# A conditional transformer block on one core: the last ssm residual gets second-level leaves, sums of the last ff residuals move ahead, the last stores are cut by column halves

## The chip, the cores and the metric

The kernel runs on one core of a Trainium2 chip. The core has a matrix engine (PE, which also loads its weights, PEld), a vector engine (DVE), a scalar engine (ACT), GpSimd (POOL) and a sync engine (SP). Each runs its own queue in program order; semaphores order them against each other. In this kernel PE writes to eight PSUM tiles ("banks") of up to 128 x 512 floats, DVE and ACT read them, and POOL works on SBUF alone. Transfers are issued from SP and ACT. The metric is device microseconds per execution, as the median of several runs.

## The reference

The input is x, 2 sequences of 2048 tokens with 512 features, and one condition vector per sequence. All is in float32:

```
emb = silu(t) @ ada_w + ada_b            # six vectors of 512 per sequence
shift_msa, scale_msa, gate_msa, shift_mlp, scale_mlp, gate_mlp = split(emb, 6)
norm = ln(x) * (1 + scale_msa) + shift_msa
h = gelu(norm @ ssm_w1 + ssm_b1)         # 512 -> 512, exact gelu
x = x + gate_msa * (h @ ssm_w2 + ssm_b2) # the "ssm residual"
norm2 = ln(x) * (1 + scale_mlp) + shift_mlp
hf = gelu_tanh(norm2 @ ff_w1 + ff_b1)    # 512 -> 1024
x = x + gate_mlp * (hf @ ff_w2 + ff_b2)  # 1024 -> 512, the "ff residual"
```

## The kernel before

**Tiling.** The 4096 tokens are cut into 8 blocks of 512 (`i` = 0 to 7). A block's x is one tile of 128 partitions x 4 token rows x 512 features. For each block there are four matmul stages, named after the tiles they write: hA (first ssm layer), oA (ssm residual), hC (first ff layer) and oC (ff residual). Names like `px_hC` or `pl_oC_P_y` are PSUM tiles of such a stage. The loop over `i` does hC_i, oA_(i+1), oC_i, hA_(i+2); block 5 ("ahead", `i + 3 == NBLK`) has the order hC_5, oA_6, hA_7, oC_5, oA_7. Blocks 6 and 7 ("alone") have hC and oC only. PE goes through all stages in one row; all other work is hooked into these stages: `hook(hooks, places, ops)` puts an operation behind a named place of a stage, and it lands in its own engine's queue in that order. The order is written out by hand (`tc.manual_schedule()`).

**Seven products instead of eight.** A matrix product cut into 2 x 2 quarters is done with seven quarter products P1 to P7, whose operands are sums and differences of quarters (`sums_of_first` for activations, `sums_of_second` for weights, four additions each; the third works in place). The results are added up in PSUM: `BANK` says which bank (y, x or v) a product goes to. After a product is complete, DVE adds the bank into the quarters of x that need it; a later product accumulates onto the same bank, and so waits until that read is done. After P1, ACT copies bank y to bank x in the `CARRIED` order. hC uses a program of 26 products (`HK_P`), whose moving operands ("registers", `forms`) are made by the 20 operations of `HK_B`, most on POOL, six of them on DVE from copies in PSUM.

**Leaves.** A product can be cut again in the same way: seven leaf products with 128-wide operands instead of four matmuls with 256-wide ones. `residual_with_leaves` (from L912) does so for oA of blocks 3 to 6: P1, P5, P6, P7 plain, and P2, P3, P4 in seven leaf rounds R0 to R6 (products in the order of `LEAVES`); a round does the same leaf of all three. Their activation operands are made by `First.leaf_sums`, eight sums, their weight operands by `leaves_of_w2`, which changes w2 in place. `plain_w2` changes it back for oA_7, which is done by `residual` (L876) with seven plain products, 28 matmuls of 128 x 256.

`residual_in_leaves` (from L977) does oC of blocks 1, 4, 6 and 7: P1 and P6 plain, P2, P3, P5, P4, P7 as leaves, each of two matmuls. Its order is P1 and its read (L1005), round R0, plain P6, rounds R1 to R6. After round 1 DVE reads P6 for the upper half of x (L1005), after round 2 for the lower half (L1092). Each round's results are added at L1056. In round 6 of the last block the order is P4, P7, P2, P3, P5. oC of blocks 2, 3 and 5 is `residual_in_all_leaves`; its adds are at L1150.

**Operands of the ff residual.** `Second.summed(1, ...)` makes the four hC sums of the second half of the ff activations (`hC_sums`), `Second.leaf_sums` the leaf operands: `sums24` (for P2, P4), `sums35` (P3, P5) and `sums7` (P7), four each. For blocks 6 and 7 `hC_sums` and `sums24` are on DVE, the others on POOL. All these additions are at L386.

**Statistics.** The normalisation of a block's x starts with `stats` (four pairs at L608 and L609), then `root` (L661 on DVE, L662 on POOL), then `steps`. Those of the last block stand partly in oA_7 and partly between the products of hC_6.

**Stores.** In the last block's oC two token rows are stored after each of the last three rounds, one from SP, one from ACT (L1103, L1106): after rounds 4 and 6 half of their columns, after round 5 whole rows.

Of the kernel before, what the change touches and what calls it, by code (L numbers as in the profile page):

```python
# [140 lines left out]
def kernel(  # L141
# [371 lines left out]
    def plain_w2(w_sb, s, eng):  # L513

        for w in (w_sb[:, KD // 2 :, :], s[:, 2]):
            v = w.rearrange("p h (q e d) -> p h q e d", e=2, d=P)
            eng.tensor_tensor(v[:, 0, :, 1], v[:, 1, :, 1], v[:, 0, :, 1], ALU.subtract)

# [393 lines left out]
    def residual_with_leaves(name, i, hops, wops, leaf_wops, hooks):  # L912
# [7 lines left out]
        rooms = {  # L920
            b: (ps_t if tag == "t" else ps_g).tile([P, 4, P], F32, tag=tag, name=f"pl_{name}_{b}")
            for b, tag in (("y", "t"), ("x", "x"), ("v", "t"))
        }
        started = set()
# [15 lines left out]
        def leaf_round(r):  # L940
            f = LEAVES[r]
            b = LEAF_BANK[f]
            for n, p in enumerate(("P2", "P3", "P4")):
                nc.tensor.matmul(
                    rooms[b][:, n, :],
                    hops.leaves[p][f],
                    leaf_wops[p][f],
                    start=b not in started,
                    stop=(f in ("P2", "P3", "P4")),
                    skip_group_check=True,  # L950
                )
                started.add(b)
            if r == 0:
                nc.scalar.copy(rooms["x"][:, :3], rooms["y"][:, :3])
                started.add("x")
                return
            t, e = LEAF_AT[f]
            for d, n in ((X[:, 0, t, :, e, :], slice(0, 2)), (X[:, 1, t, :1, e, :], slice(2, 3))):
                nc.vector.tensor_tensor(d, rooms[b][:, n], d, ALU.add)
# [17 lines left out]
    def residual_in_leaves(name, i, hops, wops, leaf_wops, kdim, hooks, last, five, carried):  # L977
# [84 lines left out]
        for r, f in enumerate(LEAVES):  # L1062
# [11 lines left out]
            if r == 0 and carried:  # L1074
                x23, x4 = rooms["P23", "x"], rooms["P4", "x"]
                nc.scalar.copy(x23[:, :2], rooms["P23", "y"][:, :2])
                nc.scalar.copy(x4[:, : 1 + five], rooms["P4", "y"][:, : 1 + five])
                if five:
                    nc.scalar.copy(x4[:, 2], seeded[:, 0])
                started |= {("P23", "x"), ("P4", "x")}  # L1080
                dests = {}
            for p in ("P5", "P4", "P7", "P3") if i + 2 == NBLK and r == 5 else on:
                if p in dests:
                    add(*dests[p])
            if five and r == 0:
                hooked("R0")
                run(plain("P6"))
                hooked("P2")
            if five and r == 1:
                read("P6", "12")  # L1090
            if five and r == 2:
                nc.vector.tensor_tensor(  # L1092
                    xt[:, 2:4, :].rearrange("p t (q d) -> p t q d", q=2),
                    ps["y"].unsqueeze(2).to_broadcast([P, 2, 2, F]),
                    xt[:, 2:4, :].rearrange("p t (q d) -> p t q d", q=2),
                    ALU.add,
                )
            if not five and r == 4:
                read("P7", "22", "21")
            if last and r >= 4:  # L1100
                for eng, row in ((nc.sync, t), (nc.scalar, 2 + t)):
                    if f == "P3":
                        eng.dma_start(out=out_blk[i][:, row, :], in_=xt[:, row, :])  # L1103
                    else:
                        cols = slice(e * P, (e + 1) * P)
                        eng.dma_start(  # L1106
                            out=out_blk[i][:, row].rearrange("p (q d) -> p q d", q=2)[:, :, cols],
                            in_=xt[:, row].rearrange("p (q d) -> p q d", q=2)[:, :, cols],
                        )
# [99 lines left out]
    class First:  # L1209
# [14 lines left out]
        def leaf_sums(self, eng):  # L1224

            flat = forms.rearrange("p n a r -> p (n a r)")[:, 18 * P : 27 * P]
            s24 = thirds(flat[:, : 6 * P].rearrange("p (s q t) -> p s q t", s=3, q=2))
            s3 = thirds(flat[:, 6 * P :].rearrange("p (s t) -> p s t", s=3))
# [387 lines left out]
    for i in range(1, NBLK):  # L1616
# [31 lines left out]
        elif nxt:  # L1648
            hook(hooks, (1, 3), last_stats[2:])
            hook(hooks, (3,), [n2[i + 1].root])  # L1650
# [37 lines left out]
        hook(hooks, EARLY, hC_sums[: 2 if alone else 4])  # L1688
# [63 lines left out]
        if alone:  # L1752
            hook(hooks, ("P1",), hC_sums[2:] + sums7[:2] + sums35[:2] + sums24[:2] + sums7[2:] + sums35[2:])
            hook(hooks, ("R0", "P6"), sums24[2:])
        if seven and nx2:
            n1_sums = hA[i + 2].summed(nc.gpsimd) if ahead else n1[i + 2].summed(nc.gpsimd)
            hook(hooks, ("0a",), [lambda: n2[i + 1].root()] + sums17[:1] + (leaf_fold or [])[:-2])
# [11 lines left out]
        elif nx2:  # L1769

            hook(hooks, ("P1",), [lambda: n2[i + 1].root()])
            hook(hooks, ("P1",), (leaf_fold or [])[:-2] + [lambda: n2[i + 1].rest(found["room"])])
# [3 lines left out]
            if leaf_fold:  # L1776
                hook(hooks, ("P5", "P7"), leaf_fold[-2:])
# [97 lines left out]
        if ahead:  # L1875
# [3 lines left out]
            plain_w2(w2_sb, w2_s, nc.vector)  # L1879
            residual(f"oA_{i + 2}", i + 2, hA[i + 2], w2_ops, KD // 2, hooks, order=CARRIED)  # L1880
# [47 lines left out]
```

## Time and profile before

| what | us |
|---|---|
| median of 3 runs (lowest, highest) | 580.98 (580.52, 581.02) |
| the profiled execution | 580.38 |
| its span, first to last instruction | 578.6 |
| PE busy in the span | 572.1 |
| DVE, POOL, ACT busy | 453.8, 432.2, 292.8 |
| oA_7 on PE | 471.5 to 483.6 |
| hC_6 and oC_6 on PE | 483.6 to 528.7 |
| hC_7 and oC_7 on PE | 528.7 to 574.5 |

The granted PE clock is full in every slice of the page. A row of the time order gives the start (us from the start of the span), the length, the engine, the line, the operation, the tiles written and read, the shape and the count; a length for several instructions runs from the first one's start to the last one's end. A bracket at the end of a row gives the idle time of the engine before it and who ended it. PE's ends are modelled and overlap the next start, so distances on PE are taken from start to start. One matmul in float32 counts as two instructions. A windows row gives, behind the window, its length, the busy time of PE, PEld, DVE, ACT and POOL with the count of instructions, the PE clock, the busy share of the DMA engines and GB/s.

### The profile page before, as it was taken

Reading aid. Unit: us, or ns where it says so; the run is one execution under the profiler, and the core shown is the slowest. Engines: PE = TensorE matmul, PEld = TensorE weight load, DVE = VectorE, ACT = ScalarE, POOL = GpSimd, SP = SyncE. Lnnn points to the kernel's source line nnn. Section 1 sums busy time; section 2 is a strip of 40 time slices with the busy share of each in tenths; the row PEclk is TensorE's granted clock in tenths of the full one; section 3 lists DMA queues with packets and bytes.
Section 4 is the critical chain, followed back from the end, with each engine's and each line's share of the span. In section 5 each row is a group of like instructions: output and inputs, shape, how many; then the busy total and the mean of one; then the engine's idle time right before and its main releaser. Section 6 shows DMA issues by size and latency. Waiting matters only on the chain.

```text
span 578.6 us, 10061 instructions
## 1 busy us (share of the span) xinstructions
PE 572.1 (99%) x3425; PEld 514.2 (89%) x3425; DVE 453.8 (78%) x955; ACT 292.8 (51%) x574; POOL 432.2 (75%) x452
## 2 busy tenths in 40 slices
PE   8999999999999999999999999999999999999997
PEld 4888888888899889998899988998898998899896
DVE  4968898996878586986869877985857597887677
ACT  3726457705652875448724688335655332731520
POOL 1665449999959869888899989998993955369351
PEclk9999999999999999999999999999999999999999
DMA  8977333204205413383032921153140250031002
GB/s 331 387 233 248 96 75 91 92 37 146 64 11 148 171 47 73 98 260 118 1 92 68 346 79 30 45 144 117 69 109 2 110 146 2 1 74 73 1 2 73
DMA packets 26831, 62.30 MB, mean 108 GB/s; under 512 B 5104, under 2 KB 6172, under 8 KB 25116
## 3 DMA queue, kind: packets, MB, share of 16 engines
q1 hardware_dynamic: 22768, 55.87, 30.0%
q10 hardware_dynamic: 4012, 5.79, 3.8%
q8 instruction: 27, 0.44, 0.3%
q14 instruction: 24, 0.20, 0.1%
HBM read 35.94 MB, written 9.97 MB: 79 GB/s over the span
## 4 chain that ended last, share of the span: by engine, by line
PE 95%; DVE 2%; DMA 2%; issue 0%; SPq 0%; DVEq 0%
PE px_hC L1281 10%; PE py_hA L571 10%; PE py_hC L1281 8%; PE pv_hC L1281 8%; PE py_oA L571 5%; PE py_oC L994 5%; PE pv_hA L571 5%; PE pl_oC_P_y L1042 4%; PE pl_oC_A_y L1132 4%; PE py_oA L929 4%; PE pl_oC_B_y L1132 3%; PE py_hC L571 2%; PE pv_oA L571 2%; PE px_hA L571 2%; PE py_oC L571 2%; PE pl_oC_P_v L1042 2%
## 5 line engine op out<-in xcount | busy, mean ns | idle before, releaser
L662 POOL TENSOR_TENSOR r<-ve,minus_half 128x4 f32<-128x4 f32 x16 | 16.6, 1038 | 56.1 <-DVE ve L661 49.3
L773 ACT ACTIVATE nT<-nT,mod,mod 128x512 f32<-128x512 f32 x32 | 23.4, 803 | 46.1 <-DMA nT<-blocks 32.2
L1205 POOL TENSOR_TENSOR forms<-forms 128x256 f32<-128x256 f32 x56 | 42.1, 751 | 4.1 <-DVE forms L1201 0.7
L1281 PE MATMUL py_hC<-forms,fw 128*128 128x256 f32 x168 | 40.9, 379 | 0.0
L1298 DVE TENSOR_TENSOR hClo<-hClo,py_hC 128x512 f32<-128x512 f32 x42 | 28.6, 684 | 11.6 <-ACT hClo L1295 8.2
L725 ACT ACTIVATE nT<-x,nmr,rstd 128x512 f32<-128x512 f32 x36 | 26.8, 804 | 19.4 <-DVE nmr L710 16.9
L1281 PEld LDWEIGHTS py_hC<-forms,fw 128*128 128x128 f32 x168 | 31.7, 190 | 4.6 <-DVE hClo L1298 0.2
L386 POOL TENSOR_TENSOR hSC<-hClo,hChi 128x512 f32<-128x512 f32 (+1 forms) x16 | 19.2, 1205 | 19.9 <-ACT hChi L1276 19.1
L608 DVE BATCH_NORM_STATS2 st<-x 128x6 f32<-128x512 f32 x42 | 28.4, 676 | 4.8 <-DMA x<-in_x_dram 4.8
L1298 DVE TENSOR_TENSOR hChi<-hChi,pv_hC 128x512 f32<-128x512 f32 x35 | 23.2, 680 | 9.4 <-PE pv_hC L1281 5.1
L1276 ACT ACTIVATE hClo<-hClo,colsT 128x256 f32<-128x256 f32 x56 | 25.3, 499 | 5.0 <-DVE hClo L1298 4.8
L1281 PE MATMUL px_hC<-forms,fw 128*128 128x256 f32 x112 | 27.6, 379 | 0.0
L773 ACT ACTIVATE x<-x,mod 128x512 f32<-128x512 f32 x24 | 17.5, 802 | 18.6 <-DMA x<-blocks 18.6
L736 DVE STREAM_TRANSPOSE blocks<-nT 128x512 f32<-128x512 f32 x36 | 24.2, 694 | 2.8 <-ACT nT L725 2.8
L1276 ACT ACTIVATE hChi<-hChi,colsT 128x256 f32<-128x256 f32 x56 | 25.1, 497 | 1.9 <-DVE hChi L1298 1.9
L386 POOL TENSOR_TENSOR hClo<-hClo 128x512 f32<-128x512 f32 (+1 forms) x23 | 26.1, 1137 | 0.0
L1295 ACT ACTIVATE hChi<-py_hC 128x512 f32<-128x512 f32 x14 | 7.6, 595 | 34.3 <-PE py_hC L1281 34.2
L1295 ACT ACTIVATE hClo<-px_hC 128x512 f32<-128x512 f32 x21 | 12.5, 596 | 22.6 <-PE px_hC L1281 19.1
L1281 PEld LDWEIGHTS px_hC<-forms,fw 128*128 128x128 f32 x112 | 21.3, 190 | 2.9
L571 PE MATMUL py_hA<-x,w 128*128 128x256 f32 x96 | 22.7, 379 | 0.0
L1298 DVE TENSOR_TENSOR hChi<-hChi,px_hC 128x512 f32<-128x512 f32 x28 | 19.0, 680 | 4.2 <-ACT hClo L1295 2.1
L1281 PE MATMUL px_hC<-forms,fw_s 128*128 128x256 f32 x84 | 20.7, 381 | 0.0
(519 smaller groups left out, 1913.3 us busy)
## 6 DMA issues: line engine op xcount, KB each, us to landing
x<-in_x_dram SPq DMA_DIRECT2D x13, 1024.0 KB
out_dram<-x SPq DMA_DIRECT2D x14, 512.0 KB
x<-blocks SPq DMA_DIRECT2D x96, 64.0 KB
nT<-blocks SPq DMA_DIRECT2D x88, 64.0 KB
ada<-in_L_cond_ada_w_dram SPq DMA_DIRECT2D x5, 1024.0 KB
fw<-in_L_cond_ff_w_dram SPq DMA_DIRECT2D x2, 2048.0 KB
nT<-blocks ACTq DMA_DIRECT2D x56, 64.0 KB
w<-in_L_cond_ssm_w_dram SPq DMA_DIRECT2D x2, 1024.0 KB
```

What stands on the lines that cost most here:

```text
L386: eng.tensor_tensor(out[:, r], a[:, r], b[:, r], f)
L571: nc.tensor.matmul(ps[b][j * apart][:, j, :], lhs(p, j, k), rhs(p, j, k), start=(fresh and j * (not apart) == 0 and k == 0), stop=(p in (" ...
L608: nc.vector.bn_stats(st, xs[self.i][:, c, :])
L725: nc.scalar.activation(t, x_c, AF.Identity, bias=self.nmr[:, c : c + 1], scale=self.rstd[:, c : c + 1])
L773: nc.scalar.activation(dst, src, AF.Identity, bias=shift, scale=scale)
L994: yield lambda j=j, k=k: nc.tensor.matmul(ps[BANK[p]][:, j, :], hops(p, j, k), wops[p][:, k, :], start=False, stop=(k == kdim - 1), skip_g ...
L1042: nc.tensor.matmul(t[:, n, :], hops.leaves[p][f][:, k, :], leaf_wops[p][f][:, k, :], start=room not in started, stop=(f in ("P2", "P3", "P ...
L1132: nc.tensor.matmul(rooms[g, b][:, at[p], :], hops.leaves[p][f][:, k, :], leaf_wops[p][f][:, k, :], start=(g, b) not in started, stop=(f in ...
L1205: eng.tensor_tensor(reg[d], reg[a], reg[b], ALU.add if f == "+" else ALU.subtract)
L1276: nc.scalar.activation(h, h, AF.Gelu_apprx_tanh, bias=fb1T[:, m : m + 1])
L1281: nc.tensor.matmul(ps[b][:, j, :], fa[ra][:, j * P : (j + 1) * P], fb[rb].rearrange("p a (c q) -> p c a q", q=Q), start=(fresh and j == 0) ...
L1298: nc.vector.tensor_tensor(dest(d), dest(d), ps[b], op)
```

## The change

- oA_7 is done by `residual_with_leaves`. Its tile for bank y has the tag x instead of t (`y_tag`), and the three tiles for the leaves are made at first use. The eight leaf sums of its activations are hooked at "6b" of oC_5, on POOL, and written into free parts of w1, of w1's sums and of the gate bias. `plain_w2` goes.
- In hC_6 the last two statistics of block 7 move from behind products 1 and 3 to behind 3 and 5, the root from behind 3 to behind 6.
- In oC_6 and oC_7 all four `hC_sums` run before the stage, so ahead of P1's read, where the last two ran behind it. All four `sums24` are at "P1", where the last two were at R0 and P6.
- In `residual_in_leaves` (blocks 1, 4, 6, 7) the lower read of P6 (L1092) moves from after round 2 to after round 1. In blocks 1 and 4 the last but one weight fold (`leaf_fold[-2]`) moves from "P5", which is behind round 2, to "P1".
- After round 6 of the last block the stores are cut by the halves q of the features: q = 0 after the adds of P3, q = 1 after those of P5, each from SP and ACT.

```diff
-    def plain_w2(w_sb, s, eng):
...
-    def residual_with_leaves(name, i, hops, wops, leaf_wops, hooks):
+    def residual_with_leaves(name, i, hops, wops, leaf_wops, hooks, y_tag="t"):
...
-        rooms = {
-            b: (ps_t if tag == "t" else ps_g).tile([P, 4, P], F32, tag=tag, name=f"pl_{name}_{b}")
-            for b, tag in (("y", "t"), ("x", "x"), ("v", "t"))
-        }
-        started = set()
+        rooms, started = {}, set()
+
+        def room(b):
+            if b not in rooms:
+                tag = {"y": y_tag, "x": "x", "v": "t"}[b]
+                rooms[b] = (ps_t if tag == "t" else ps_g).tile([P, 4, P], F32, tag=tag, name=f"pl_{name}_{b}")
+            return rooms[b]
...
+            def leave_columns(qs):
+                for eng, row in ((nc.sync, t), (nc.scalar, 2 + t)):
+                    cols = slice(e * P, (e + 1) * P)
+                    eng.dma_start(
+                        out=out_blk[i][:, row].rearrange("p (q d) -> p q d", q=2)[:, qs, cols],
+                        in_=xt[:, row].rearrange("p (q d) -> p q d", q=2)[:, qs, cols],
+                    )
+
             for p in ("P5", "P4", "P7", "P3") if i + 2 == NBLK and r == 5 else on:
                 if p in dests:
                     add(*dests[p])
+                if last and r == 6 and p in ("P3", "P5"):
+                    leave_columns(slice(p == "P5", 1 + (p == "P5")))
...
-            if five and r == 2:
+            if five and r == 1:
                 nc.vector.tensor_tensor(
                     xt[:, 2:4, :].rearrange("p t (q d) -> p t q d", q=2),
                     ps["y"].unsqueeze(2).to_broadcast([P, 2, 2, F]),
...
-            if last and r >= 4:
+            if last and r == 4:
+                leave_columns(slice(0, 2))
+            if last and r == 5:
                 for eng, row in ((nc.sync, t), (nc.scalar, 2 + t)):
+                    eng.dma_start(out=out_blk[i][:, row, :], in_=xt[:, row, :])
...
-        def leaf_sums(self, eng):
+        def leaf_sums(self, eng, parts=None):
...
+            if parts is None:
+                flat = forms.rearrange("p n a r -> p (n a r)")[:, 18 * P : 27 * P]
+                parts = [flat[:, n * P : (n + 2) * P] for n in (0, 2, 4)] + [flat[:, n * P : (n + 1) * P] for n in (6, 7, 8)]
+            s24, s3 = [r.rearrange("p (q t) -> p q t", q=2) for r in parts[:3]], parts[3:]
...
-            hook(hooks, (1, 3), last_stats[2:])
-            hook(hooks, (3,), [n2[i + 1].root])
+            hook(hooks, (3, 5), last_stats[2:])
+            hook(hooks, (6,), [n2[i + 1].root])
...
-        hook(hooks, EARLY, hC_sums[: 2 if alone else 4])
+        hook(hooks, EARLY, hC_sums)
...
         if alone:
-            hook(hooks, ("P1",), hC_sums[2:] + sums7[:2] + sums35[:2] + sums24[:2] + sums7[2:] + sums35[2:])
-            hook(hooks, ("R0", "P6"), sums24[2:])
+            hook(hooks, ("P1",), sums7[:2] + sums35[:2] + sums24 + sums7[2:] + sums35[2:])
         if seven and nx2:
             n1_sums = hA[i + 2].summed(nc.gpsimd) if ahead else n1[i + 2].summed(nc.gpsimd)
+            if ahead:
+                first = w1_s[:, 0].rearrange("p k d -> p (k d)")
+                parts = [leaf_flat[:, 6 * W : 7 * W], leaf_flat[:, 7 * W :], first[:, :W]]
+                parts += [first[:, W : W + P], first[:, W + P :], gb[2][:, :P]]
+                last_leaf_sums = hA[i + 2].leaf_sums(nc.gpsimd, parts)
+                hook(hooks, ("6b",), last_leaf_sums)
...
-            hook(hooks, ("P1",), (leaf_fold or [])[:-2] + [lambda: n2[i + 1].rest(found["room"])])
+            hook(hooks, ("P1",), (leaf_fold or [])[:-2] + [lambda: n2[i + 1].rest(found["room"])] + (leaf_fold or [])[-2:-1])
...
-                hook(hooks, ("P5", "P7"), leaf_fold[-2:])
+                hook(hooks, ("P7",), leaf_fold[-1:])
...
-            plain_w2(w2_sb, w2_s, nc.vector)
-            residual(f"oA_{i + 2}", i + 2, hA[i + 2], w2_ops, KD // 2, hooks, order=CARRIED)
+            residual_with_leaves(f"oA_{i + 2}", i + 2, hA[i + 2], w2_ops, w2_leaf, hooks, "x")
```

18 lines of the change are left out of this document (2 added, 16 removed).

## The prediction

> **What bounds the kernel now.** I read the page first, for who is busy over the whole span.
>
> ```profile
> span 578.6 us, 10061 instructions
> ...
> PE 572.1 (99%) x3425; PEld 514.2 (89%) x3425; DVE 453.8 (78%) x955; ACT 292.8 (51%) x574; POOL 432.2 (75%) x452
> ```
>
> The matrix engine (PE) is busy 99% of the span, so a change gains only by giving PE less to do, by closing small waits between its matmuls, or by shortening what follows its last matmul. A busy share of 99% hides small waits, because a matmul that waits is drawn longer. So I next read PE in order of time and compared equal pieces of work. A last-layer residual (oC) ends with four leaf rounds R3 to R6 of fixed size; from the start of R4 to the next stage three rounds pass. In block 6 (first two rows) they take 528.70 - 522.00 = 6.70 us, so one round is 2.23 us. The other pairs are the same distance in blocks 1, 4 and 7 (for block 7 from the start of R4 to its last product, which is 0.45 short of the end).
>
> ```profile
> 522.00 0.61 PE L1042 MATMUL pl_oC_P_y<-fw,hChi 128*128 128x128 f32 x4
> ...
> 528.70 1.03 PE L1281 MATMUL py_hC<-forms,fw_s 128*128 128x256 f32 x4
> ...
> 179.09 0.61 PE L1042 MATMUL pl_oC_P_y<-fw,hChi 128*128 128x128 f32 x4
> ...
> 186.09 1.89 PE L571 MATMUL py_hA<-x,w 128*128 128x256 f32 x8
> ...
> 384.21 0.61 PE L1042 MATMUL pl_oC_P_y<-fw,hChi 128*128 128x128 f32 x4
> ...
> 391.31 1.89 PE L571 MATMUL py_hA<-x,w 128*128 128x256 f32 x8
> ...
> 566.99 0.61 PE L1042 MATMUL pl_oC_P_y<-fw,hChi 128*128 128x128 f32 x4
> ...
> 573.90 0.61 PE L1042 MATMUL pv_oC<-fw_t,hSC 128*128 128x128 f32 x4
> ```
>
> Block 1 needs 7.00 (0.30 lost), block 4 needs 7.10 (0.40 lost), block 7 needs 6.91 where 6.70 - 0.45 = 6.25 would do (0.66 lost; 0.45 is a fifth of 2.23, one product of a round). What is late there is the vector engine (DVE), which adds each round into x and so frees the bank. Its order of time in block 7:
>
> ```profile
> 554.81 0.69 DVE L1005 TENSOR_TENSOR x<-py_oC,x 128x512 f32<-128x512 f32 x1 [1.24 <-PE py_oC L994]
> ...
> 556.01 0.68 DVE L386 TENSOR_TENSOR hSC<-hChi,hSC 128x512 f32<-128x512 f32 x1
> ...
> 558.89 1.75 DVE L386 TENSOR_TENSOR hChi<-hChi 128x512 f32<-128x512 f32 x1
> 561.45 0.42 DVE L1056 TENSOR_TENSOR x<-pl_oC_P_x,x 128x256 f32<-128x256 f32 x1 [0.82 <-PE pl_oC_P_x L1042]
> 562.78 1.08 DVE L1056 TENSOR_TENSOR x<-pl_oC_P_x,x 128x256 f32<-128x256 f32 x3 [0.90 <-PE pl_oC_P_x L1042]
> ...
> 564.38 1.76 DVE L386 TENSOR_TENSOR forms<-hChi,forms 128x512 f32<-128x512 f32 x1
> ...
> 567.70 1.22 DVE L1092 TENSOR_TENSOR x<-py_oC,x 128x1024 f32<-128x1024 f32 x1
> ...
> 574.62 0.42 DVE L1056 TENSOR_TENSOR x<-pv_oC,x 128x256 f32<-128x256 f32 x1
> ```
>
> The brackets are idle time: DVE idles 1.24 + 0.82 + 0.90 = 2.96 us before 562.78 and, by this view, never after it. A leaf sum of 1.76 us stands in the full stretch, at 564.38. From there DVE trails PE by more than a round until the end. Last I read the tail by windows:
>
> ```profile
> 575.10:575.90 0.80, 0.00 (x0) 0.00 (x0) 0.00 (x0) 0.00 (x0) 0.00 (x0) 1.00 0.10 21
> 575.90:577.00 1.10, 0.00 (x0) 0.00 (x0) 0.00 (x0) 0.00 (x0) 0.00 (x0) 1.00 0.87 238
> 577.00:578.60 1.60, 0.00 (x0) 0.00 (x0) 0.00 (x0) 0.00 (x0) 0.00 (x0) 0.99 0.00 0
> ```
>
> The last two numbers are DMA share and GB/s. The last add ends at 574.62 + 0.42 = 575.04. About 0.9 us later the last two stores move, for 0.87 x 1.10 = 0.96 us, and 1.6 us of nothing closes the span.
>
> **Part 1: the last ssm residual with leaves.** Before, it is seven plain products from 471.48 to 483.57. The same residual one block earlier already has the leaves, from 425.92 to 437.51.
>
> ```profile
> 425.92 1.89 PE L929 MATMUL py_oA<-w,hA 128*128 128x256 f32 x8
> ...
> 437.51 0.81 PE L571 MATMUL py_hA<-x,w 128*128 128x256 f32 x3
> ```
>
> ```profile
> 471.48 1.89 PE L571 MATMUL py_oA<-w,hA 128*128 128x256 f32 x8
> ...
> 483.57 0.59 PE L1281 MATMUL py_hC<-forms,fw_s 128*128 128x256 f32 x2
> ```
>
> 12.09 against 11.59: 0.50 us less on PE, if nothing new waits. A plain product is 12.09 / 7 = 1.73; a leaf round is (11.59 - 4 x 1.73) / 7 = 0.67.
>
> New work on GpSimd (POOL): eight leaf sums of the activations. The same eight stand one block earlier, from 414.96 to 419.20 + 0.46, so 4.70 us. They come behind the sum that ends at 464.86 + 1.29 = 466.15 and end at 470.85.
>
> ```profile
> 414.96 0.73 POOL L386 TENSOR_TENSOR forms<-hA 128x256 f32<-128x256 f32 x1
> ...
> 419.20 0.46 POOL L386 TENSOR_TENSOR forms<-hSA,forms 128x128 f32<-128x128 f32 x1
> ...
> 464.86 1.29 POOL L386 TENSOR_TENSOR hSA<-hA,hSA 128x512 f32<-128x512 f32 x1
> 472.06 0.73 POOL L1205 TENSOR_TENSOR forms<-nT 128x256 f32<-128x256 f32 x1 [5.91 <-ACT nT L773]
> ...
> 473.55 0.92 POOL L1205 TENSOR_TENSOR forms<-nT 128x256 f32<-128x256 f32 x1
> ```
>
> Behind them in POOL's queue are the register sums ("forms") of the next stage, which start at 472.06 for another reason (ScalarE). POOL idles 5.91 us there, so 4.70 fit with 1.2 to spare: cost nothing.
>
> DVE in this residual:
>
> ```profile
> 430.31 1.22 DVE L938 TENSOR_TENSOR x<-pv_oA,x 128x1024 f32<-128x1024 f32 x1 [1.72 <-PE pv_oA L929]
> 431.67 0.62 DVE L959 TENSOR_TENSOR x<-pl_oA_x,x 128x256 f32<-128x256 f32 x2
> ...
> 471.68 1.48 DVE L1150 TENSOR_TENSOR x<-pl_oC_B_y,x 128x256 f32<-128x256 f32 x5 [0.25 <-PE pl_oC_B_y L1132]
> ...
> 474.63 1.54 DVE L1201 TENSOR_TENSOR forms<-copy,forms 128x256 f32<-128x256 f32 x4
> 476.09 0.75 DVE L1201 TENSOR_TENSOR nT<-copy,nT 128x256 f32<-128x256 f32 x2
> ```
>
> The two subtractions that restored plain weights (between 473.16 and 474.63) go; their time is not PE's. The six form differences cannot start before POOL's third form (473.55 + 0.92 = 474.47), and they then take the 2.21 between 474.63 and 476.84; I let them end at 476.84, as before. Then come P5's add (1.22), R1's and R2's (0.62 each). R2's first read, of 0.42, is done by 476.84 + 1.22 + 0.62 + 0.4 = 479.1. R4 overwrites that bank at 471.48 + 3 x 1.73 + 4 x 0.67 = 479.35. That is a margin of 0.25: no wait, but a thin one. The new bank for round 0 is the one that oC of block 5 leaves at 471.68 + 1.48 = 473.16; round 0 starts at 471.48 + 1.73 = 473.21. I take 0.45 of the 0.50, and 0.2 to 0.65 for the range, since the next stage has one wait that the moved statistics may remove or renew (two pairs of statistics, two products later; the first user of them, the scale steps from product 8 on, stays put):
>
> ```profile
> PEld px_hC L1281 <- DVE hChi L1298: 0.3, 1, 0.3
> ```
>
> Making the bank tiles at first use moves no instruction in the four earlier residuals with leaves: nothing.
>
> **Part 2: DVE order in blocks 6 and 7.** The hC sums [2] and [3] (0.68 each) move ahead of P1's read, into the 1.24 us idle before 554.81; P1's read stays. The other two of the four DVE leaf sums move from R0 and P6 to behind P1's read. In block 7 the four then run from 554.81 + 0.69 = 555.5: the first two take 558.89 - 556.69 = 2.2, then 1.75 and 1.76, end near 561.2; the next add can start at 561.45 anyway. The 1.76 leaves 564.38, and L1092's 1.22 moves up into its place. R1's adds end at 562.78 + 1.08 = 563.86, P6's two reads (0.69 and 1.22) at 565.8, and from there four adds of at most 0.42 (1.7) against 2.23 of PE per round let DVE catch up before R6. PE gains the 0.66 lost above; the last add (0.72 after the start of PE's last product) moves with it. I take 0.65, with 0.3 to 0.75 for the range. What is late next is PE itself.
>
> Block 6 has no wait to remove, but its round 0 adds now stand behind all four leaf sums:
>
> ```profile
> 511.63 1.22 DVE L386 TENSOR_TENSOR leaves<-hChi 128x512 f32<-128x512 f32 x1
> ...
> 513.91 0.41 DVE L1056 TENSOR_TENSOR x<-pl_oC_P_y,x 128x256 f32<-128x256 f32 x1
> ...
> 519.33 0.74 DVE L386 TENSOR_TENSOR leaves<-hChi,leaves 128x512 f32<-128x512 f32 x1
> ```
>
> Two sums take 513.91 - 511.63 = 2.28. With the other two at 1.75 and 0.74 the first add starts at 516.4 and is read by 516.8; R2 writes that bank at 522.00 - 2 x 2.23 = 517.54. No wait. At the dearest row (1.76) for all four it is read at 511.63 + 7.04 + 0.41 = 519.08, a wait of 1.5: the upper bound.
>
> The Trainium skill, page "SBUF — State Buffer", section "Who interferes with whom", says that a DVE instruction with both inputs in SBUF contends with a GpSimd instruction that reads SBUF, and that one with a single SBUF input does not. The trace agrees: this sum takes 0.74 in one place and 1.76 in another, while the adds from PSUM stay at 0.42. Four sums in a row beside POOL's eight is where that rule speaks against the change; by it the sum would lose the 1.5 of the upper bound.
>
> **Part 3: blocks 1 and 4** share the function, so there too L1092's read moves from round 2 to round 1, and one weight fold moves from "P5" (behind L1092) up to "P1". In block 1 that fold was:
>
> ```profile
> 179.39 1.45 DVE L386 TENSOR_TENSOR fw<-fw 128x256 f32<-128x256 f32 x1
> ```
>
> It stood ahead of R3's adds and made R4 and R5 late. At P1 it lies in the wait for the transposes. So 0.30 in block 1; in block 4 I take 0.30 of 0.40, since R2's first read is now behind 1.22 of L1092. Range 0.2 to 0.7 for both.
>
> **Part 4: the stores.** The last two stores become four, each pair half as long. The first pair leaves one add earlier, and the last pair has half of 0.96 to move: 0.48 less. I take 0.45, with -0.1 (a second issue in the same queue) to 0.5.
>
> The Trainium skill, page "DMA: Bandwidth & Descriptors", section "Measured (HBM→SBUF, 128 partitions, SWDGE, issued from GpSimd)", calls transfers under 64 KB descriptor-dominated, which speaks against cutting; its fit of 436 GB/s would give, as an estimate, 0.30 for the 128 KB taken off the last pair. The 0.96 measured here for 256 KB goes ahead of it.
>
> **Sum.** 0.45 + 0.65 + 0.30 + 0.30 + 0.45 = 2.15 us. The profiled execution took 580.38, the median of the runs is 580.98, 0.6 above it. I put the gain on the median: 578.8.
>
> **Rivals.**
> - *The cut store buys nothing* (its fixed 0.9 + 1.6 is most of it): 580.98 - 1.70 = 579.3. For it: only 0.96 of 3.5 us moves bytes. Against: the bytes do end last.
> - *R4 of blocks 1 and 4 now waits for L1092* instead of the fold: 579.4. Against: the fold was as long, and is gone.
> - *DVE and POOL hold each other up*, so that block 6's four sums take the upper bound: 2.15 - 1.5, 580.3. For it: 1.75 and 1.76. Against: 0.74 in block 6.
> - *Slower: the leaf sums start late on POOL.* They write into tiles of w1 and the gate bias that other instructions of oC still use. If they are held until that stage is over (471.48 instead of 466.15), the forms start at 476.2, the third ends at 478.6, DVE's six differences behind it at 481.0, and R4 of the ssm residual waits until 483.2 instead of 479.35: 3.9 lost, 582.7. It costs from 1.5 of delay on (1.2 of POOL's slack plus 0.25), eats the gain at 3.6, and shows as slower from 4.8, a start after 471. Against it: at 414.96 such sums wrote to "forms" while the matmuls of that hC stage, which ends at 425.92, still read other parts of it.
>
> **Chances.** 0.2% is 1.16 us, about what a measurement of this kernel can tell from no change. Forecast 0.55, store rival 0.12, R4 rival 0.08 (all under 579.82: faster 0.75), sums rival 0.14 (within 0.2%), late sums 0.11 (slower). Range: all high ends (0.65 + 0.75 + 0.7 + 0.5 = 2.6) from the profiled time give 577.8; the sums rival gives 580.3. So 577.8 to 580.4, leaving out the late sums.
>
> **What would show it.** Part 1: the residual takes 11.6 on PE, POOL's leaf sums lie between 466 and 471, and the next stage starts 0.4 to 0.5 sooner. Part 2: no leaf sum on DVE after 562, DVE idle again between rounds 4 and 6, and PE 6.25 from R4 to its last product. Part 3: 6.7 instead of 7.0 and 7.1. Part 4: DMA busy about half a microsecond after the last issue has started to move. It is wrong if PE waits for DVE in a new place: at R4 of the ssm residual, or at R2 of block 6.

## The result, and the profile after

| what | before | after |
|---|---|---|
| median of 6 runs each, us | 580.43 (580.19 to 581.02) | 577.80 (577.64 to 578.15) |
| the profiled execution | 580.38 | 577.74 |
| its span | 578.6 | 575.9 |

The ratio is 0.9953, with a 95% interval of 0.994 to 0.9966: faster, by 2.63 us. The forecast was 578.8, so the direction held and the gain was larger than the 2.15 worked out. The span lost 2.7 us.

From the page of the changed kernel, its span, its busy times and the shares of the chain that ended last:

```profile
span 575.9 us, 10119 instructions
...
PE 570.8 (99%) x3443; PEld 514.1 (89%) x3443; DVE 453.6 (79%) x963; ACT 292.7 (51%) x574; POOL 436.7 (76%) x460
...
PE 97%; DMA 2%; SPq 0%; DVE 0%; issue 0%; DVEq 0%
```

And from the page of the kernel before, the same shares:

```profile
PE 95%; DVE 2%; DMA 2%; issue 0%; SPq 0%; DVEq 0%
```

PE is still the bound. It has 18 instructions more and 1.3 us less of drawn time, POOL has eight sums more (4.5 us). DVE, which the prediction found in the way, is at 0% of the chain, where it had 2%.

PE in order of time (start, length, engine, line and operation), at the places that the prediction compared. Lines have shifted by a few: L1042 is now L1038, L1056 is L1052, L1092 is L1098.

```profile
179.02 0.61 PE L1038 MATMUL pl_oC_P_y<-fw,hChi 128*128 128x128 f32 x4
...
185.72 1.46 PE L565 MATMUL py_hA<-x,w 128*128 128x256 f32 x6
...
383.96 0.68 PE L1038 MATMUL pl_oC_P_y<-fw,hChi 128*128 128x128 f32 x4
...
390.74 1.46 PE L565 MATMUL py_hA<-x,w 128*128 128x256 f32 x6
...
470.91 1.89 PE L925 MATMUL py_oA<-w,hA 128*128 128x256 f32 x8
...
478.77 0.39 PE L940 MATMUL pl_oA_y<-w,hA 128*128 128x128 f32 x2
...
482.51 1.03 PE L1283 MATMUL py_hC<-forms,fw_s 128*128 128x256 f32 x4
...
565.78 0.61 PE L1038 MATMUL pl_oC_P_y<-fw,hChi 128*128 128x128 f32 x4
...
572.03 0.61 PE L1038 MATMUL pv_oC<-fw_t,hSC 128*128 128x128 f32 x4
```

From R4 to the next stage block 1 now takes 6.70 (7.00 before) and block 4 takes 6.78 (7.10). The ssm residual takes 482.51 - 470.91 = 11.60 (12.09); its R4 starts at 478.77, without a wait. Block 7 takes 6.25 from R4 to its last product (6.91).

POOL's leaf sums for this residual, the first and the last of eight:

```profile
465.50 0.74 POOL L386 TENSOR_TENSOR w<-hA 128x256 f32<-128x256 f32 x1
...
469.74 0.46 POOL L386 TENSOR_TENSOR gb<-hSA,w_s 128x128 f32<-128x128 f32 x1
```

They end at 470.20, ahead of the stage.

DVE in block 7, from the fourth leaf sum on:

```profile
557.62 1.76 DVE L386 TENSOR_TENSOR forms<-hChi,forms 128x512 f32<-128x512 f32 x1
560.24 0.42 DVE L1052 TENSOR_TENSOR x<-pl_oC_P_x,x 128x256 f32<-128x256 f32 x1 [0.86 <-PE pl_oC_P_x L1038]
...
563.16 1.22 DVE L1098 TENSOR_TENSOR x<-py_oC,x 128x1024 f32<-128x1024 f32 x1
...
570.45 1.08 DVE L1052 TENSOR_TENSOR x<-pl_oC_P_v,x 128x256 f32<-128x256 f32 x3 [0.91 <-PE pl_oC_P_v L1038]
...
572.76 0.42 DVE L1052 TENSOR_TENSOR x<-pv_oC,x 128x256 f32<-128x256 f32 x1
```

The slow leaf sum lies ahead of 560, L1098 is early, and at 570.45 DVE waits for PE again (0.91), where before it never idled after 562.78.

The tail by windows (length, busy times and counts, PE clock, DMA share, GB/s). The last add ends at 572.76 + 0.42 = 573.18.

```profile
573.10:573.90 0.80, 0.00 (x0) 0.00 (x0) 0.09 (x1) 0.00 (x0) 0.00 (x0) 1.00 0.86 200
573.90:574.60 0.70, 0.00 (x0) 0.00 (x0) 0.00 (x0) 0.00 (x0) 0.00 (x0) 1.00 0.70 193
574.60:575.90 1.30, 0.00 (x0) 0.00 (x0) 0.00 (x0) 0.00 (x0) 0.00 (x0) 1.00 0.00 0
```

From the last add to the end of the span it takes 575.90 - 573.18 = 2.72 us. Before it took 578.60 - 575.04 = 3.56.

Where the 2.7 us came from, by the lengths of the stages on PE from start to start (stages that the edits leave alone, such as hC_1, oC_6 and hC_7, agree to 0.02 in all profiles):

| place | before | after | gain | forecast |
|---|---|---|---|---|
| all ahead of oC_1 | | | 0.07 | - |
| oC_1 | 22.84 | 22.54 | 0.30 | 0.30 |
| oC_4 | 22.94 | 22.74 | 0.20 | 0.30 |
| oA_7 | 12.09 | 11.60 | 0.49 | 0.45 |
| hC_6 | 22.60 | 22.45 | 0.15 | in the range of oA_7 |
| oC_6 | 22.53 | 22.53 | 0 | 0 |
| oC_7, R4 to last product | 6.91 | 6.25 | 0.66 | 0.65 |
| last add to end | 3.56 | 2.72 | 0.84 | 0.45 |
| sum | | | 2.71 | 2.15 |

### The profile page after: what moved, and what is told of

Read it like the earlier page. It is cut to its first block, busy times and chain, and to the rows that moved or that the text cites. A ratio compares the mean times of both kernels' runs of the same rounds, so it can differ in the third digit from the quotient of the medians.

```text
span 575.9 us, 10119 instructions
## 1 busy us (share of the span) xinstructions
PE 570.8 (99%) x3443; PEld 514.1 (89%) x3443; DVE 453.6 (79%) x963; ACT 292.7 (51%) x574; POOL 436.7 (76%) x460
## 4 chain that ended last, share of the span: by engine, by line
PE 97%; DMA 2%; SPq 0%; DVE 0%; issue 0%; DVEq 0%
PE px_hC L1283 11%; PE py_hA L565 10%; PE py_hC L1283 8%; PE pv_hC L1283 8%; PE pl_oC_P_y L1038 5%; PE py_oC L990 5%; PE pv_hA L565 5%; PE py_oA L925 5%; PE pl_oC_A_y L1133 4%; PE py_oA L565 4%; PE pl_oC_P_v L1038 3%; PE pl_oC_B_y L1133 3%; PE py_hC L565 2%; PE px_hA L565 2%; PE py_oC L565 2%; PE pl_oA_y L940 2%
## 5 line engine op out<-in xcount | busy, mean ns | idle before, releaser
L1297 ACT ACTIVATE hChi<-py_hC 128x512 f32<-128x512 f32 x14 | 7.6, 594 | 34.0 <-PE py_hC L1283 14.8
```

## The experiments

Diffs are against the changed kernel where nothing else is said; "..." stands for lines left out. The lengths of stages named are those of the table above. Where no range is given the kernel ran once. The changed kernel's own runs lie between 577.64 and 578.15, so for these the lengths of the stages decide, and the time alone can't tell half a microsecond.

### The stores

**The last stores in one piece per row again:**

```diff
-                if last and r == 6 and p in ("P3", "P5"):
-                    leave_columns(slice(p == "P5", 1 + (p == "P5")))
...
-            if last and r == 4:
+            if last and r in (4, 6):
```

> The changed kernel with the last round's stores uncut again (one per queue, after P5's add). PE and DVE should be as in the changed kernel: the last product starts at 572.0, the last add ends at 573.2. Theory A (the cut itself is worth the whole 0.84 us between last add and end): the end is 3.56 us after the last add again, span 576.7. Rival B (only the half of the bytes counts, 0.45, and the rest of the 0.84 came with the earlier end of the row stores before it): 3.1 to 3.2 us after the last add, span 576.35.

Measured: 578.61 us over 5 runs (578.48 to 578.91), ratio to before 0.9964 (0.995 to 0.9978), span 577.1. The last add ends at 573.57. The tail by windows:

```profile
573.57:574.50 0.93, 0.00 (x0) 0.00 (x0) 0.01 (x1) 0.00 (x0) 0.00 (x0) 1.00 0.07 16
574.50:575.50 1.00, 0.00 (x0) 0.00 (x0) 0.00 (x0) 0.00 (x0) 0.00 (x0) 1.00 0.93 261
575.50:577.10 1.60, 0.00 (x0) 0.00 (x0) 0.00 (x0) 0.00 (x0) 0.00 (x0) 1.00 0.00 0
```

The tail is 3.53 again, and the stages of the table are as in the changed kernel, so the cut alone is worth 0.81 between these two profiles, and 578.61 - 577.80 = 0.81 in the medians: theory A. (The last add ends 0.39 later than in the changed kernel; 0.22 of that is there when oC_1 starts.) Its parts: the same 0.9 until bytes move, 1.0 of bytes instead of about 0.5, and 1.6 instead of 1.3 after the last byte.

**Only the last pair, and only the first pair of round 6:**

```diff
-                    leave_columns(slice(p == "P5", 1 + (p == "P5")))
+                    if p == "P5":
+                        leave_columns(slice(1, 2))
```

(and the other one with "P3" and slice(0, 1)). Each of the two leaves a part of the output unstored.

> The changed kernel without the first pair of stores of round 6 (the left halves of the columns of the last two rows and column half are not stored, so that part of the output is missing). Theory A (the last pair starts when its own add is done, and the pair in front of it only takes its bytes out of the way): from the end of the last add to the end of the span 2.7 us as in the changed kernel, span 575.8 to 576.0. Theory B (the last pair still stands behind the bytes of the first pair and of round 5, whose transfers keep all engines of the queue full from 572.0 to 573.5): its bytes move earlier, at most 0.4, and the tail is 2.3 to 2.5.

> The changed kernel without the last pair of stores of round 6 (the right halves of the columns of the last two rows and column half are not stored, so that part of the output is missing). It tells what part of the tail is fixed. Theory A (every store costs a fixed time after its last byte, 1.3 to 1.6 us, whatever stands behind it): the first pair's bytes are through by about 573.9, so the span ends near 575.2 to 575.4, 0.5 to 0.7 less than 575.9. Theory B (the end is set by something else than the last stores, such as the vector engine's last add and the closing of the program): 575.8 to 575.9 still.

Measured: 578.10 us without the first pair; the last add ends at 573.42 and the span at 576.3, a tail of 2.88. 577.91 us without the last pair; the last add ends at 573.73 and the span at 576.1, a tail of 2.37. Windows of these two kernels, from the last add on:

```profile
574.00:575.00 1.00, 0.00 (x0) 0.00 (x0) 0.00 (x0) 0.00 (x0) 0.00 (x0) 1.00 0.47 131
575.00:576.30 1.30, 0.00 (x0) 0.00 (x0) 0.00 (x0) 0.00 (x0) 0.00 (x0) 0.56 0.00 0
```

```profile
573.70:574.50 0.80, 0.00 (x0) 0.00 (x0) 0.04 (x1) 0.00 (x0) 0.00 (x0) 1.00 0.83 181
574.50:576.10 1.60, 0.00 (x0) 0.00 (x0) 0.00 (x0) 0.00 (x0) 0.00 (x0) 1.00 0.00 1
```

With no pair ahead of it the last pair ends no sooner (2.88 against 2.72): theory A there, the first pair costs the last one nothing. With no last pair at all the tail is only 0.35 shorter than 2.72. That is less than the 0.5 to 0.7 of theory A for that kernel, though its mechanism held: after the first pair's last byte 1.6 us pass here too. That pair was issued up to 0.5 before the last add's end (572.76 from ACT, 573.23 from SP) and moves bytes until 574.5, so this run does not show how long a tail without any store would be. Over all kernels with cut stores and both pairs the tail lay between 2.72 and 2.97, in the two with uncut ones it was 3.53 and 3.56. The part after the last byte was 1.6 in both uncut ones and between 1.3 and 1.6 in those with cuts, so its 0.3 is not shown to belong to the cut.

### The ssm residual

**Plain products in oA_7 again** (with `plain_w2` before it, without the leaf sums on POOL, statistics at their new places):

```diff
...
-            residual_with_leaves(f"oA_{i + 2}", i + 2, hA[i + 2], w2_ops, w2_leaf, hooks, "x")
+            plain_w2(w2_sb, w2_s, nc.vector)
+            residual(f"oA_{i + 2}", i + 2, hA[i + 2], w2_ops, KD // 2, hooks, order=CARRIED)
```

> The changed kernel with the last ssm residual as seven plain products again (plain weights restored on DVE, no leaf sums on POOL, first bank as before), the statistics still at their new places. Theory A: the residual takes 12.09 us on PE again instead of 11.60, and the next stage still has no wait, so the span is 0.49 longer, 576.4. Rival B: the 0.15 us that the next stage lost before came from the plain residual, not from the places of the statistics, and comes back too: 576.55.

Measured: 578.3 us, span 576.5; oA_7 takes 12.09, hC_6 stays at 22.44. The leaves are worth 0.49, and the 0.15 of hC_6 is not theirs: theory A.

**The statistics of block 7 at their old places:**

```diff
-            hook(hooks, (3, 5), last_stats[2:])
-            hook(hooks, (6,), [n2[i + 1].root])
+            hook(hooks, (1, 3), last_stats[2:])
+            hook(hooks, (3,), [n2[i + 1].root])
```

> The changed kernel with the last statistics in hC_6 at their old places (behind products 1 and 3, the root behind 3). Theory A (the moved statistics took the 0.15 out of hC_6: an eviction of hC_6 by the vector engine stood behind them and the matrix engine waited 0.3 for it): hC_6 is 22.60 again instead of 22.45, with a weight load that waits for the vector engine's eviction; span 576.0 to 576.1. Theory B (the 0.15 came from the residual in front of it, which now ends with the vector engine less far behind): hC_6 stays 22.45, span 575.9.

Measured: 578.89 us, span 577.1; hC_6 takes 23.24, which is 0.79 more, not 0.15. Theory A named the mechanism, but missed its size. PE at the product that waits, and DVE ahead of it:

```profile
488.94 1.13 PE L1283 MATMUL px_hC<-forms,fw_s 128*128 128x256 f32 x4
490.47 1.13 PE L1283 MATMUL px_hC<-forms,fw_s 128*128 128x256 f32 x4 [0.40 <-DVE hChi L1300]
```

```profile
486.72 0.69 DVE L602 BATCH_NORM_STATS2 st<-x 128x6 f32<-128x512 f32 x1
487.44 0.18 DVE L603 BATCH_NORM_AGGREGATE mv<-st 128x2 f32<-128x6 f32 x1
487.54 0.66 DVE L1300 TENSOR_TENSOR hChi<-hChi,px_hC 128x512 f32<-128x512 f32 x1
488.11 0.69 DVE L602 BATCH_NORM_STATS2 st<-x 128x6 f32<-128x512 f32 x1
488.83 0.18 DVE L603 BATCH_NORM_AGGREGATE mv<-st 128x2 f32<-128x6 f32 x1
489.05 0.17 DVE L655 TENSOR_SCALAR ve<-mv 128x4 f32<-128x4 f32 x1
489.13 0.69 DVE L1300 TENSOR_TENSOR hClo<-hClo,py_hC 128x512 f32<-128x512 f32 x1
489.74 0.68 DVE L1300 TENSOR_TENSOR hChi<-hChi,px_hC 128x512 f32<-128x512 f32 x1
```

The eviction that frees bank x starts at 489.74 behind two pairs of statistics. In the kernel before, the same one started at 489.79:

```profile
489.62 2.04 PE L1281 MATMUL px_hC<-forms,fw_s 128*128 128x256 f32 x8
```

```profile
489.79 0.68 DVE L1298 TENSOR_TENSOR hChi<-hChi,px_hC 128x512 f32<-128x512 f32 x1
```

PE came to this product 0.68 later then (489.62 against 488.94) and lost 0.15. With the leaves PE is there earlier, and DVE is not: its rows show no idle time from 481.73 until that eviction ends. So the wait takes the gain back: without the moved statistics the leaf residual would have brought a small loss (0.49 gained in oA_7, 23.24 - 22.60 = 0.64 lost in hC_6).

**Four idle sums on POOL ahead of the leaf sums** (of 128x512, written where the leaf sums write afterwards):

```diff
-                hook(hooks, ("6b",), last_leaf_sums)
+                idle_sum = lambda: nc.gpsimd.tensor_tensor(leaf_flat[:, 6 * W :], hA[i + 2].lo[:, 0], hA[i + 2].lo[:, 1], ALU.add)
+                hook(hooks, ("6b",), [idle_sum] * 4 + last_leaf_sums)
```

> The changed kernel with four idle sums of 128x512 on GpSimd ahead of the leaf sums of the last ssm residual (4 x 1.28 = 5.1 us), so that these end near 475.3 instead of 470.2 and the sums for hC_6 start near 475.4 instead of 471.57, 3.8 later. Theory A (the prediction's slower rival as a mechanism: the vector engine's six differences wait for the third of those sums, and P5's add and the reads of R1 and R2 stand behind them in its queue): R4 of the residual waits for R2's read, about 3.8 less a margin of 0.6, so oA_7 is 15.3 instead of 11.60 and the span about 579.1. Theory B (PE goes on, since the sums are wanted only by hC_6 from 482.5 on): oA_7 stays within 0.3 of 11.60, span 575.9 to 576.3. Theory C (hC_6 is late as well, because all its operands come 3.8 later): more than 3.2 is lost, part of it as waits in hC_6.

Measured: 584.15 us, span 582.4, oA_7 takes 18.01 instead of 11.60. POOL, DVE, PE, and three windows over PE's waits:

```profile
465.51 5.34 POOL L1763 TENSOR_TENSOR w<-hA 128x512 f32<-128x512 f32 x4
...
475.57 0.73 POOL L1206 TENSOR_TENSOR forms<-nT 128x256 f32<-128x256 f32 x1
```

```profile
477.81 1.42 DVE L1202 TENSOR_TENSOR forms<-copy,forms 128x256 f32<-128x256 f32 x4 [4.22 <-POOL forms L1206]
```

```profile
479.61 0.49 PE L940 MATMUL pl_oA_v<-w_t,w 128*128 128x128 f32 x2 [1.35 <-DVE nT L1202]
...
482.36 0.80 PE L940 MATMUL pl_oA_y<-w,hA 128*128 128x128 f32 x2 [1.81 <-DVE x L955]
...
488.92 1.03 PE L1283 MATMUL py_hC<-forms,fw_s 128*128 128x256 f32 x4
```

```profile
480.30:482.36 2.06, 0.25 (x4) 0.06 (x2) 1.93 (x6) 0.00 (x0) 1.90 (x3) 0.70 0.00 0
482.36:488.00 5.64, 5.64 (x18) 4.92 (x19) 2.33 (x6) 0.00 (x0) 4.98 (x8) 0.50 0.00 1
488.00:489.00 1.00, 1.00 (x11) 1.00 (x10) 1.00 (x3) 0.00 (x0) 0.00 (x0) 1.00 0.00 0
```

The chain is theory A's: POOL's sums for hC_6 start 4.0 later, DVE's differences wait for them, and the reads of the residual stand behind. PE waits twice. R3 waits for the bank that the differences read, R4 for the read of R2. From R4 to hC_6 it should then take 482.51 - 478.77 = 3.74, as in the changed kernel; it takes 488.92 - 482.36 = 6.56. So of the 6.41 lost, 2.82 come after the waits, on a halved clock, and 6.41 - 2.82 = 3.59 are the waits: in slices of 0.1 us the granted clock falls to 0.50 at about 481.1 and is back at about 488.0. hC_6 itself takes 22.45, so theory C's waits there did not come. The 3.59 of waits are 0.4 more than theory A's 3.8 less 0.6 (3.2, so its oA_7 should have read 14.8 and not 15.3); the rest of the loss is the clock.

The Trainium skill, page "TensorE: Matmul & The Clock Gate", section "Part 1: The HAM clock gate", gives half rate after at least one idle window of about 3.4 us and full rate after about 3.4 us of sustained work, in windows that run free of the kernel. The factor of two agrees with the 0.50 here. So does the return, although the clock stayed low for 5.6 us of unbroken work: 6.9 us at half rate is near two such windows (6.8, an estimate from the page's 3.4), and PE still waited in the first of them. The fall agrees only in part: PE worked for about 1.1 of the 3.0 us between 478.10 and the fall, so the window ahead of it was not wholly idle.

### Block 7

**The order of DVE's sums as before in blocks 6 and 7:**

```diff
-        hook(hooks, EARLY, hC_sums)
+        hook(hooks, EARLY, hC_sums[: 2 if alone else 4])
...
-            hook(hooks, ("P1",), sums7[:2] + sums35[:2] + sums24 + sums7[2:] + sums35[2:])
+            hook(hooks, ("P1",), hC_sums[2:] + sums7[:2] + sums35[:2] + sums24[:2] + sums7[2:] + sums35[2:])
+            hook(hooks, ("R0", "P6"), sums24[2:])
```

> The changed kernel with the DVE order of the sums in blocks 6 and 7 as before (two hC sums behind P1's read, two leaf sums at R0 and P6), but the lower read of P6 still after round 1. Theory A (the leaf sum in the full stretch is what held PE in block 7): the 0.66 us comes back, R4 to last product 6.9 us, span 576.55. Rival B (the earlier lower read was the cure): R4 to last product stays at 6.25 us, span 575.9. If the lower read now stands behind the leaf sum, both before R2's adds, PE may lose up to 1.2 us.

**The lower read of P6 behind round 2 as before** (in blocks 1, 4, 6 and 7):

```diff
-            if five and r == 1:
+            if five and r == 2:
                 nc.vector.tensor_tensor(
```

> The changed kernel with the lower read of P6 after round 2 again, in blocks 1, 4, 6 and 7. Theory A (that move is not needed once the sums and the fold are out of the way): block 7 keeps 6.25 us from R4 to the last product, block 1 keeps 6.70, and block 4 gets better, since R4 no longer waits behind that read (four rounds R3 to R6 take 9.13 now, 8.93 without a wait): span 575.7 to 575.9. Rival B (the move is what freed the rounds): block 7 loses 0.4 to 0.7, blocks 1 and 4 0.2 to 0.4 each, span 576.5 or more.

**Both:**

> The changed kernel with both moves of block 7 undone together: the order of the vector engine's sums in blocks 6 and 7, and the lower read of P6 (after round 2 again). Each alone left oC_7 at 25.96 to 26.0 us and the three rounds from the start of R4 to the last product at 6.25. Theory A (either move is enough, the wait returns only when both are gone): from R4 to the last product 6.9 us again, the leaf sum in front of round 3 takes 1.76 beside a sum of GpSimd, the span is about 576.6 to 576.7 less what the read gains in block 4 (0.16), so 576.4 to 576.6. Theory B (neither is the cause, something else of the change gave the 0.66, the leaf residual or the cut stores): 6.25 still, span 575.8 to 576.1.

Measured: 577.78 us with the old order, 577.93 with the old read, 578.68 with both old. From R4 to the last product it takes 6.25, 6.26 and 6.91. So theory A for the first run fell (undoing the order alone was to bring the wait back), theory A of the second and of the third hold: either move is enough. DVE's last leaf sum of block 7, in the kernel with the old order, with POOL's last sum:

```profile
564.34 0.68 DVE L386 TENSOR_TENSOR forms<-hChi,forms 128x512 f32<-128x512 f32 x1
```

```profile
563.15 1.28 POOL L386 TENSOR_TENSOR forms<-hSC,forms 128x512 f32<-128x512 f32 x1
```

and in the kernel with both old, with POOL beside it:

```profile
563.27 1.78 DVE L386 TENSOR_TENSOR forms<-hChi,forms 128x512 f32<-128x512 f32 x1
```

```profile
561.99 1.27 POOL L386 TENSOR_TENSOR hSC<-hSC 128x512 f32<-128x512 f32 x1
563.23 1.26 POOL L386 TENSOR_TENSOR forms<-hSC,forms 128x512 f32<-128x512 f32 x1
```

In the first of the two the lower read (1.21 there) stands ahead of the sum, which so starts as POOL's last sum ends (564.34 against 563.15 + 1.28 = 564.43) and takes 0.68.

**Both old, and POOL's last two sums of block 7 left out** (against the kernel with both old; two operands of the last block are then not made):

```diff
-            hook(hooks, ("P1",), hC_sums[2:] + sums7[:2] + sums35[:2] + sums24[:2] + sums7[2:] + sums35[2:])
+            hook(hooks, ("P1",), hC_sums[2:] + sums7[:2] + sums35[:2] + sums24[:2] + sums7[2:] + sums35[2 : 2 if i == NBLK - 1 else 4])
```

> The kernel in which both moves of block 7 are undone (from round 4 to the last product 6.91 us, the vector engine's leaf sum at 563.27 takes 1.78 while GpSimd does two sums of 128x512 beside it), now without these two GpSimd sums in block 7 (two of the leaf operands for P3 and P5 of the last block are then not made, so its output is wrong). Theory A (the two engines slow each other, and the 1.1 us that this costs the vector engine is the wait): the leaf sum takes 0.7, from round 4 to the last product 6.25, span about 576.1 to 576.3 instead of 576.9. Theory B (the sum is slow by itself, from its operands' places, or the wait comes from its place in the order alone): it takes 1.7 to 1.8 again and the rounds 6.9; or it takes 0.7 and the rounds still need over 6.7.

Measured: 577.74 us, span 575.9. R4 starts at 565.78 and the last product at 572.03, so 6.25, with DVE's order of before:

```profile
563.17 0.68 DVE L386 TENSOR_TENSOR forms<-hChi,forms 128x512 f32<-128x512 f32 x1
```

Theory A: the 1.10 that POOL's sums cost this one DVE sum was the whole wait of block 7. PE was not held up by POOL's two sums themselves: in the kernel with both old, the one wait that is listed for it in these rounds (0.2, of a weight load) is for DVE's adds. The Trainium skill, page "SBUF — State Buffer", section "Who interferes with whom", has a rule for this (a DVE instruction with two SBUF inputs contends with a GpSimd instruction that reads SBUF); here it holds with 0.68 without POOL's sums and 1.78 beside them.

### Blocks 1 and 4

**The weight fold behind round 2 as before** (in blocks 1 and 4):

```diff
-            hook(hooks, ("P1",), (leaf_fold or [])[:-2] + [lambda: n2[i + 1].rest(found["room"])] + (leaf_fold or [])[-2:-1])
+            hook(hooks, ("P1",), (leaf_fold or [])[:-2] + [lambda: n2[i + 1].rest(found["room"])])
...
-                hook(hooks, ("P7",), leaf_fold[-1:])
+                hook(hooks, ("P5", "P7"), leaf_fold[-2:])
```

> The changed kernel with the last but one weight fold of blocks 1 and 4 behind round 2 again (its lower read of P6 stays after round 1). Theory A (as the prediction had it: the fold in front of round 3's adds was the cause of the lost 0.30 and 0.40): oC_1 is 22.8 instead of 22.54 and oC_4 22.9 or more instead of 22.74, span 576.3 to 576.5. Theory B (as in block 7: one move out of that stretch is enough): oC_1 stays 22.54; oC_4 stays 22.74 or gets a little shorter, because the early read then no longer stands behind the fold; span 575.7 to 575.9.

**The lower read behind round 2 in block 4 alone:**

```diff
-            if five and r == 1:
+            if five and r == (2 if i == 4 else 1):
```

> The changed kernel with the lower read of P6 behind round 2 again in block 4 alone (the weight fold stays at P1). Undoing it everywhere made oC_4 22.58 instead of 22.74 us and left oC_1 (22.54) and oC_7 (25.96) as they were. Theory A (in block 4 the early read itself stands in front of rounds 1 and 2 on a vector engine that is still late from the fold and the transposes, so round 4 waits for it): oC_4 22.58, span 0.16 less, 575.7, and the time 577.6 or within 0.03% of the changed kernel's 577.8. Theory B (the 0.16 came with the later start of that run's whole sequence, not from the read): oC_4 22.74, span 575.9.

Measured: the old fold gives 578.04 us, the old read in block 4 gives 577.75 over 4 runs (577.55 to 577.81; ratio to before 0.9952, 0.9934 to 0.997). With the runs that had the old read everywhere (the lower read alone, both moves of block 7 undone, and the same without POOL's sums) these are all four cases:

| | oC_1 | oC_4 |
|---|---|---|
| both old (before) | 22.84 | 22.94 |
| old fold, new read | 22.54 | 22.86 |
| new fold, old read | 22.54 | 22.57 to 22.59 |
| both new (after) | 22.54 | 22.74 |

In block 1 either move is enough, as in block 7 (theory B of the first run). In block 4 the fold's move alone brings 0.36 and the read's move then takes 0.16 back: theory A of the second run, and of the first run neither, since 22.86 lies between its two. DVE in block 4 of the changed kernel, and in the kernel with the old read there:

```profile
382.27 1.22 DVE L1098 TENSOR_TENSOR x<-py_oC,x 128x1024 f32<-128x1024 f32 x1
383.40 0.41 DVE L1052 TENSOR_TENSOR x<-pl_oC_P_y,x 128x256 f32<-128x256 f32 x1
```

```profile
382.66 0.42 DVE L1052 TENSOR_TENSOR x<-pl_oC_P_y,x 128x256 f32<-128x256 f32 x1
```

The first read of bank y in that round ends at 383.40 + 0.41 = 383.81 when L1098 stands ahead of it, and R4, which writes there, starts at 383.96. In the other kernel it ends at 383.08 and R4 does not wait. This version has the shortest oC_4, but 0.15 of 577.8 can't be told in the medians (577.75 against 577.80).

## Why the prediction was right or wrong

The step that failed is the price of part 4: its term gave the cut stores 0.45, with 0.5 as the most, and the tail lost 0.84 (0.81 came back with the cut alone undone). The other three parts ended within their own ranges (0.64 with hC_6, 0.66, 0.50), so with the 0.07 ahead of oC_1 the span gained 2.71, more than the 2.6 of all four high ends together. A second step, the time that the gain was taken from, put the forecast higher still.

- **Part 1, right, a little low.** 0.49 of the 0.50 arrived at oA_7 (0.45 was taken). POOL's leaf sums lay from 465.5 to 470.2, as forecast, and R4 did not wait. What fell short is the side remark on the moved statistics, taken as one that "may remove or renew" a wait of 0.3. They removed a loss of 0.15, and kept away one of 0.79. The argument lacked that DVE, whose queue is full there, does not get to hC_6's evictions earlier when PE does.
- **Part 2, right in size (0.66 against 0.65), half right in cause.** DVE's leaf sum of 1.76 was the cause, and POOL's sums beside it were why. The prediction took the two moves together; each alone removes the wait. In block 6 no wait came. The four sums took 0.68, 1.10, 1.75 and 1.75 there, so the slow length did come twice, and the last one, 0.74 before, was one of them. But the prediction let the first start as before (10.37 ahead of R4), and with the two hC sums out of its way it started 11.15 ahead: bank y was read by 515.14, and R2 wrote to it at 516.33.
- **Part 3, 0.50 of 0.60.** Block 1 gave its 0.30. For block 4 the 0.30 of 0.40 was right in kind (R2's first read is behind L1092's 1.22) and too high: 0.20. There the rival "R4 now waits" came true in part.
- **Part 4, the step that failed: 0.84 measured, 0.45 forecast.** The bytes' share was priced well (about 1.0 to about 0.5). Put at nothing was a change in the part after the last byte: it took 1.3 instead of 1.6. That difference is not shown to come from the cut, since kernels with cut stores lie anywhere from 1.3 to 1.6, so the cause of this share of the miss stays open; by the tails (2.72 to 2.97 against 3.53 and 3.56) the cut is worth 0.56 to 0.84, above the 0.5 in any case. The second issue in the same queue, the low end of -0.1, cost nothing that these tails show. The estimate from the Trainium skill's page "DMA: Bandwidth & Descriptors" (0.30, from the fit of 436 GB/s in its section "Anatomy of one DMA — SWDGE (gpsimd) path") was too low for the bytes' share as well, about 0.5 here, and cutting to stores of 64 KB did no harm that a run here shows.
- **The base.** "I put the gain on the median: 578.8" used the median of three runs, 580.98. The six runs now beside the changed kernel are these three and three more (580.19 to 580.35), and have 580.43, next to the profiled execution's 580.38. That is 0.55 of the 1.0 by which the forecast was too high; the other 0.48 is 2.63 - 2.15. From the profiled time the same sum would have given 580.38 - 2.15 = 578.2. No run shows why two of the first three were slower, and that the profiled execution lay near the later median is luck as far as is known.
- **The rivals.** "The cut store buys nothing" fell (0.56 to 0.84). "DVE and POOL hold each other up" in block 6 fell as a time, since oC_6 is 22.53 in both, though two of the four sums were held up. "The leaf sums start late" did not happen. Where it was brought about, with 5.4 us of delay, the waits (3.6) were near what it priced (5.4 less 1.45 is 3.95), but the total was 6.4, because the clock was not in the account.

## What to carry to other kernels

When PE is made faster in one stage, look at the next one for an engine whose order has no slack: here the gain of 0.49 stood or fell with two statistics that were moved by two products. The same DVE sum with both inputs in SBUF took 0.68 us where it started as GpSimd's sums ended and 1.78 beside them, so its place in the order decides what it costs. A median of three runs is a thin base for a forecast of 0.4%: it stood 0.55 too high here, and three more runs showed it.

## What the runs showed of the hardware beyond this

- The granted clock halved for 6.9 us (481.1 to 488.0) after PE had been kept waiting for about 1.9 of 3.0 us, and it cost 2.8 us on top of 3.6 us of waiting. A wait of 0.4 (the one in hC_6 with the old statistics) did nothing of the kind: the clock stayed at 1.00. The delay of such a fall is not fixed: after PE's last product, by its drawn end, the clock fell 2.1 us later in that kernel, 3.1 in the one with both moves undone, and 4.1 in the kernel before.
- With the last pair of 64 KB stores left out the tail was 2.37, with it 2.72 to 2.97. Of the tail with the last pair about 0.9 lies between the last add and that pair's first byte, about 0.5 moves bytes, and 1.3 to 1.6 follow the last byte.
- What stays open: why the part after the last byte differs by 0.3 between kernels whose last stores are alike (1.3 in the changed kernel, about 1.55 in the one with both moves undone).
